# Pacing the second image's layer work by its matmuls in a selective-scan stack

## The chip, the core and the metric

The kernel runs on one core of one Trainium2 chip, in float32. The metric is the device time of one execution, in microseconds (us). A core has engines that run side by side and meet through semaphores: PE (TensorE, matmuls; its weight loads are the row PEld), DVE (VectorE), ACT (ScalarE), POOL (GpSimd) and SP (SyncE), which here only issues DMAs. Each engine works through its own list of instructions in the order in which the program wrote them.

## What is computed

Four layers run on an input of 4 images of 64 x 64 pixels and 128 channels. Layers 0, 1 and 3 are selective-scan blocks; layer 2 is a gated block without a scan. Cut to what matters, a scan layer is:

```python
xz = layer_norm(x) @ in_proj                      # 128 -> 2 x 256 channels: x_, z
xs = silu(conv3x3_depthwise(x_) + conv_b)         # read in 4 directions k: rows, columns, and both backwards
dts, B, C = split(x_proj[k] @ xs[k])              # 8 + 16 + 16 rows for each of the 4096 positions
delta = softplus(dt_w[k] @ dts + dt_b)
h[t] = exp(delta[t] * A) * h[t-1] + delta[t] * xs[t] * B[t]   # 256 channels x 16 states
y[t] = sum over the 16 states of h[t] * C[t]
x = x + out_proj @ (layer_norm(sum over k of y) * silu(z))
x = x + fc2 @ gelu(fc1 @ layer_norm(x))
```

The rest of this text calls the recurrence for h "the scan", delta * xs * B "the B product", and h * C "the C product".

## The kernel before, in words

**Turns.** Images are taken in pairs. Each image passes the three scan layers, which makes 12 turns (`turns`): images 0 and 1 through layer 0, then both through layer 1, then layer 3, then the same for images 2 and 3. A turn scans one image in one layer. It has 4 directions x 8 chunks of 512 positions = 32 chunks, and a chunk has 8 periods, each for 4 of the 16 states of one half of the channels. There are 12 x 32 x 8 = 3072 periods.

**A period.** In each period DVE runs 4 scans (L870), two of them fed by a B product that PE makes in PSUM (`pair_db`, L845, tile `dbp`) and two by products that DVE makes itself (L983, L984) from a copy `dv` that ACT lifts into PSUM (L862). ACT computes the decays `da` (L854) and the diagonal matrices `diag` (L837) that PE uses for the next B product. POOL multiplies by C (L882) and in every second period adds two results (L884). PE sums over the states into `yp` (L895). The rows of B and C come by DMA, broadcast to all partitions (`bb`, `cb`, L821), two buffers each. The B product of the next period stands in PE's list between the two halves of a period.

**The other image's work.** Everything else of a layer (the norms, the projections, the convolution by 9 matmuls for each half of the channels, the gated block) is done for the other image while this one is scanned, in PE, ACT, DVE and POOL slots between the scan's instructions. The function `between` writes it as a list S of small steps: one step is a matmul, or an activation, or a DMA, and empty steps (`rest`) stand where a result needs time to arrive. The list from layer 1 to layer 3 holds layer 2 too; it is called gated, it is the longest, it takes 3 taps of the convolution in one step where the other lists take 1, and it has fewer empty steps (`breath` is 0 in it, so that no empty step stands between `root`, `scale` and `affine` of a norm).

**The places.** A period has four places at which `other(number)` may run steps: after the first scan, after the second scan with PE's B product and sums, after the third scan, and at the end. A turn has 32 x 32 = 1024 places. A list is spread evenly: at each place `other` runs as many steps as the share of the list's length that the share of places gone by asks for. An empty step counts as one step, as does a step with three matmuls. Lists of the first chunks of the program and of the last 7 chunks and the tail are given one chunk each.

**Queues and buffers around it.** All matmul results of the other image go through one PSUM buffer (`gap`), so that a matmul waits until the result before it has been read. A norm is the chain `mean` (PE L226), `centre` (DVE L230), `square` (ACT L234), `variance` (PE L238), `root` (ACT L241, L242), `scale` (DVE L245), `affine` (ACT L252); the norm of y (L338 to L361) is like it. A convolution ends with ACT's `take` (L413), then comes `silu` (L421), which changes ACT's function table twice. Column stores (L430) and row stores (L435) stand in SP's list with the `bb` and `cb` loads.

Of the kernel before, what the change touches and what calls it, by code (L numbers as in the profile page):

```python
# [59 lines left out]
VSS_AT, VSS_N = _columns(_VSS)  # L60
GATE_AT, GATE_N = _columns(_GATE)


@with_exitstack
def vss_stack_kernel(ctx: ExitStack, tc: tile.TileContext, x: bass.AP, weights, out: bass.AP, n_batch=B, layers=(0, 1, 2, 3)):
# [90 lines left out]
    def combine(i, psums):  # L156
# [33 lines left out]
        for m in range(2):  # L190
            S.extend((partial(turn, m), take))
            for t in range(0, 9, 4):
                count = min(4, 9 - t)
                S.extend((partial(taps, m, t, count), partial(project, count), partial(leave, m, t, count)))
        return S

    def between(e, frm, to, psums):
# [10 lines left out]
        def rest(n=pause):  # L208

            S.extend([lambda: None] * n)  # L210

# [10 lines left out]
        def norm(src, dst, wgt, bias, eps):  # L222

            def mean():
                z.ps = bank()
                nc.tensor.matmul(z.ps, mean128, src(), start=True, stop=True)  # L226
# [5 lines left out]
            def square():  # L232
                z.sq = gap1.tile([P, CH], F32, tag="sq", name="sq")
                nc.scalar.activation(z.sq, z.cen, AF.Square)  # L234

            def variance():
                z.ps = bank()
                nc.tensor.matmul(z.ps, mean128, z.sq, start=True, stop=True)  # L238
# [70 lines left out]
        def begin(c):  # L309


            def turn():
                z.ps = bank()
                for j in range(4):
                    nc.tensor.transpose(z.ps[:, j * P : (j + 1) * P], z.xt[:, j, :], ident)

            def take():
                z.res = gap2.tile([P, CH], F32, tag="res", name="res")
                nc.scalar.copy(z.res, z.ps)

            S.append(turn)
            if c + 1 < NCH:
                S.append(lambda: fetch_x(c + 1))
            S.append(take)
            later(lambda: nc.sync.dma_start(out=lane.res[:, cols(c)], in_=z.res))

        def output_norm(c):
            if to is None:
                S.append(lambda: fetch(c))
                rest(2)  # L330

            def mean():
                z.y, z.res = z.next_y, z.next_res
# [9 lines left out]
            def square():  # L343
                z.wide = gap1.tile([P, 4, CH], F32, tag="wide", name="wide")
                nc.scalar.activation(z.wide[:, 0:2], z.y, AF.Square)

            def variance():
                z.ps = bank()
# [25 lines left out]

        def project_z():
            def first():
                z.ps = bank()
                nc.tensor.matmul(z.ps, z.in_z[:, :P], z.xn, start=True, stop=True)

            def second():  # L380
                z.ps = bank()
# [7 lines left out]
        def convolve(c):  # L389

            stride = 3 if gated else 1
            for m in range(2):
                for first in range(0, 9, stride):

                    def taps(m=m, first=first):
                        if m == 0 and first == 0 and (frm is None or gated):
# [46 lines left out]
        def mixer_out(c):  # L443
            def gate():
                nc.gpsimd.tensor_mul(z.y, z.y, z.wide[:, 0:2])

            def project():
                z.ps = bank()
# [16 lines left out]
        def mlp(c, store):  # L465
# [5 lines left out]
            for j in range(4):  # L471

                def up(j=j):
                    if j == 0:
# [15 lines left out]
            for j in range(4):  # L490

                def down(j=j):
                    if j == 0:
# [50 lines left out]

        def finish(c):
            def turn():
                z.ps = bank()
# [14 lines left out]
        def gate_sums(c):  # L562
# [7 lines left out]
            norm(lambda: z.res, fresh, g["n1w"], g["n1b"], eps6)  # L570

            def first():
                z.ps = bank()
                nc.tensor.matmul(z.ps, g["w1"][:, :P], z.t, start=True, stop=True)

            def take():
                z.g1 = gap1.tile([P, CH], F32, tag="cen", name="g1")
                nc.scalar.activation(z.g1, z.ps, AF.Identity, scale=g["wdw"][:, 0:1], bias=g["cb"][:, 0:1])

            def second():  # L580
                z.ps = bank()
# [17 lines left out]
        def attention():  # L599
            g = wt[2]  # L600

            def mean():
                z.mean = gap1.tile([P, 1], F32, tag="mean", name="mean")
                nc.vector.tensor_reduce(z.mean, z.sums, AX.X, ALU.add)
                nc.vector.tensor_scalar_mul(z.mean, z.mean, 1.0 / L)

            def se():
                z.ps = bank()
# [11 lines left out]
        def gate_rest(c):  # L620
            g = wt[2]

            def project():
                z.s, z.res = z.next_s, z.next_res
# [16 lines left out]
            norm(lambda: z.res, fresh, g["n2w"], g["n2b"], eps6)  # L641

            def first():
                z.ps = bank()
                nc.tensor.matmul(z.ps, g["wf1"][:, :P], z.t, start=True, stop=True)

            def take():
                z.c1 = gap1.tile([P, CH], F32, tag="cen", name="c1")
                nc.scalar.activation(z.c1, z.ps, AF.Identity, bias=g["bf1"][:, 0:1])

            def second():
                z.ps = bank()
                nc.tensor.matmul(z.ps, g["wf1"][:, P:], z.t, start=True, stop=True)

            def both():
                z.c2 = gap1.tile([P, CH], F32, tag="sq", name="c2")
                nc.vector.scalar_tensor_tensor(z.c2, z.ps, g["bf1"][:, 1:2], z.c1, ALU.add, ALU.mult)

            def down():
                z.ps = bank()  # L660
# [95 lines left out]
    def scans(pool, ring, deep, psum):  # L756
# [178 lines left out]
        for at, (s, i) in enumerate(periods):  # L935
            then = periods[at + 1] if at + 1 < len(periods) else None
            if i == 0:
# [4 lines left out]
                if at % (8 * per_turn) == 0:  # L942
                    segments = [(steps, len(steps), frm, to) for steps, frm, to in meanwhile(s.turn)]

# [5 lines left out]
            def other(number):  # L950

                gone = at % (8 * per_turn) * 4 + number
                for todo, count, frm, to in segments:
                    while todo and count - len(todo) < count * (gone - frm) / (to - frm):
                        todo.pop(0)()

# [48 lines left out]
            if then and then[0].turn != s.turn:  # L1005
                assert not any(todo for todo, *_ in segments)
        save(*before, 1)
        add_up(*before, 0)
        add_up(*before, 1)
        while full:  # L1010
            leave(*full.pop(0))
        for todo, *_ in segments:
            for step in todo:
                step()
# [93 lines left out]
```

## Time and profile before

| what | value |
|---|---|
| median of 3 runs | 22745.52 us (22731.7 to 22749.28) |
| the profiled execution | 22741.48 us |
| its span, first to last instruction | 22739.6 us |
| busy: PE, DVE, POOL, ACT | 19888.1, 19492.9, 19252.4, 18595.2 us (87, 86, 85, 82%) |
| before the first scan; after the last period's first scan, to the end | 164.9 us; 87.1 us |
| a chunk without work of the other image | 50.7 us |
| mean granted TensorE clock | 0.959 of full speed |

The page's rows give, for a group of instructions, its line, engine, operation and tiles (out<-in), the busy time and the mean ns of one, and then the idle time of the engine just before them with what ended it. A float32 matmul shows as two PE records. Because all four engines are busy for more than four fifths of the span, no single row names the limit; the waits between the engines do.

### The profile page before, as it was taken

To read this page: it belongs to the slowest core of one execution; us is meant where nothing else is said; L and a number is where in the kernel's file an instruction comes from. 1 tells how busy PE (TensorE), PEld (TensorE's weight loads), DVE (VectorE), ACT (ScalarE), POOL (GpSimd) and SP (SyncE) were. 2 spreads that over 40 slices of the span, in tenths; PEclk is the share of its full clock that TensorE was granted. 3 is DMA by queue.
4 is the path that set the end of the run, shared out by engine and by line. 5 is a ranking of instruction groups with operands and counts; after the bars stand their busy time and mean duration, and the time that the engine had idled before them with its cause. 6 is when DMAs were issued, how large, how long until landed. Compare 5 with 4: busy or idle time off the path is not lost. (4 is left out here: it accounts for less than half of the span.)

```text
span 22739.6 us, 217018 instructions
## 1 busy us (share of the span) xinstructions
PE 19888.1 (87%) x58234; PEld 10543.0 (46%) x58234; DVE 19492.9 (86%) x20186; ACT 18595.2 (82%) x40022; POOL 19252.4 (85%) x8862
## 2 busy tenths in 40 slices
PE   7898898898888888888888888888988888888887
PEld 3444444444444444444444444444444444444443
DVE  5999888888887887888899898898888878878996
ACT  5888888888887887788788788888888878878887
POOL 5999888888887887888889888898888878878996
PEclk8999999999999999999999999999999999999999
DMA  4444444444334434434533544444443443344333
GB/s 106 151 146 149 133 135 146 134 135 144 128 130 129 133 128 124 141 132 139 139 139 138 137 142 138 133 148 133 135 143 126 128 131 134 126 129 143 137 136 106
DMA packets 2437559, 3060.10 MB, mean 135 GB/s; under 512 B 1753840, under 2 KB 1790064, under 8 KB 2238192
## 3 DMA queue, kind: packets, MB, share of 16 engines
q1 hardware_dynamic: 2436336, 3046.22, 42.5%
q8 instruction: 472, 7.73, 0.1%
q14 instruction: 751, 6.15, 0.1%
HBM read 2784.41 MB, written 261.49 MB: 134 GB/s over the span
## 5 line engine op out<-in xcount | busy, mean ns | idle before, releaser
L882 POOL TENSOR_TENSOR hc<-h,cb 128x1024 f32<-128x1024 f32 x6144 | 14411.8, 2361 | 3101.8 <-DVE h L870 1904.4
L895 PE MATMUL yp<-hc,ident 128*128 128x512 f32 x18432 | 9102.8, 621 | 661.2 <-POOL hc L884 447.5
L854 ACT ACTIVATE da<-delta,w 128x512 f32<-128x512 f32 x12288 | 8149.0, 713 | 684.1 <-DVE h L870 671.8
L870 DVE TENSOR_TENSOR_SCAN h<-da,state,dbp 128x512 f32<-128x512 f32 x5376 | 6574.0, 1261 | 1384.8 <-PE dbp L845 1100.3
L845 PE MATMUL dbp<-diag,duT 128*128 128x256 f32 x24576 | 6143.1, 394 | 1314.4 <-DVE h L870 1178.4
L870 DVE TENSOR_TENSOR_SCAN h<-da,state,dv 128x512 f32<-128x512 f32 x5376 | 6585.5, 1263 | 0.0
L845 PEld LDWEIGHTS dbp<-diag,duT 128*128 128x128 f32 x24576 | 4686.5, 195 | 3725.0 <-issue 2165.5
L895 PEld LDWEIGHTS yp<-hc,ident 128*128 128x128 f32 x18432 | 3488.9, 197 | 5003.4 <-issue 3651.1
L837 ACT ACTIVATE diag<-ident,bt 128x128 f32<-128x128 f32 x12288 | 3952.1, 401 | 0.0
L884 POOL TENSOR_TENSOR hc<-hc 128x1024 f32<-128x1024 f32 x1536 | 3621.9, 2358 | 120.4
L983 DVE TENSOR_TENSOR dv<-dv,bb 128x512 f32<-128x512 f32 x3072 | 2087.0, 679 | 837.9 <-ACT dv L862 704.4
L862 ACT COPY dv<-du 128x512 f32<-128x512 f32 x3072 | 1799.9, 586 | 1137.5 <-DVE h L870 1129.4
L984 DVE TENSOR_TENSOR dv<-dv,bb 128x512 f32<-128x512 f32 x3072 | 2116.5, 689 | 0.0
L402 PE MATMUL gap<-halo,cw 128*128 128x512 f32 x3456 | 1657.1, 604 | 17.3 <-ACT wide L385 6.8
L870 DVE TENSOR_TENSOR_SCAN h<-da,dbp 128x512 f32<-128x512 f32 x768 | 893.5, 1201 | 203.1 <-PE dbp L845 166.5
L788 PE MATMUL ps_dt<-xd,dt_w 8*128 8x512 f32 x1536 | 888.7, 659 | 147.6 <-ACT delta L791 78.5
L805 POOL TENSOR_TENSOR du<-delta,xs 128x512 f32<-128x512 f32 x768 | 978.5, 1274 | 32.7 <-ACT delta L793 32.7
L402 PEld LDWEIGHTS gap<-halo,cw 128*128 128x128 f32 x3456 | 641.1, 192 | 743.9 <-issue 697.3
L878 ACT COPY state<-h 128x2 f32<-128x2 f32 x5376 | 964.6, 179 | 0.0
L870 DVE TENSOR_TENSOR_SCAN h<-da,dv 128x512 f32<-128x512 f32 x768 | 894.7, 1203 | 0.0
L413 ACT ACTIVATE wide<-gap,w 128x512 f32<-128x512 f32 x192 | 131.9, 687 | 826.1 <-PE gap L402 826.1
L813 ACT COPY duT<-ps_duT 128x512 f32<-128x512 f32 x768 | 440.9, 574 | 182.6 <-PE ps_duT L811 181.2
(122 smaller groups left out, 11955.2 us busy)
## 6 DMA issues: line engine op xcount, KB each, us to landing
cb<-xd_d SPq DMA_DIRECT2D x1536, 1024.0 KB
bb<-xd_d SPq DMA_DIRECT2D x1536, 512.0 KB
xs<-x_row_d SPq DMA_DIRECT2D x192, 512.0 KB
xs<-x_col_d SPq DMA_DIRECT2D x192, 512.0 KB
x_col_d<-down SPq DMA_DIRECT2D x192, 256.0 KB
x_row_d<-wide SPq DMA_DIRECT2D x96, 512.0 KB
y_d<-y_sb SPq DMA_DIRECT2D x96, 512.0 KB
y<-y_d SPq DMA_DIRECT2D x96, 512.0 KB
```

The lines of the kernel that those rows point to most:

```text
L402: nc.tensor.matmul(z.ps, z.cw[:, m, t, :], z.halo[c][:, dy : dy + RPC, dx : dx + W], start=(t == 0), stop=(t == 8),)
L805: nc.gpsimd.tensor_mul(s.du[:, m], s.delta[:, m], s.xs[:, m])
L837: nc.scalar.activation(s.diag[q][:, t, :, j], ident, AF.Copy, scale=s.bt[:, t, CQ * q + j : CQ * q + j + 1])
L845: nc.tensor.matmul(s.db[:, t * P : (t + 1) * P, :], s.duT[:, t, m, :], s.diag[q][:, t], start=True, stop=True)
L854: nc.scalar.activation(da[:, j], s.delta[:, m], AF.Exp, scale=s.v["a"][:, s.k, m, n : n + 1])
L862: nc.scalar.copy(dv[i % 2], s.du[:, place(s, i)[1]])
L870: nc.vector.tensor_tensor_scan(s.h[i, side][:, j, s.step], da[:, j, s.step], db[:, s.step], init, ALU.mult, ALU.add)
L882: nc.gpsimd.tensor_mul(hc, s.h[i, side], s.cb[i // 2][:, 2 * side : 2 * side + 2, :])
L884: nc.gpsimd.tensor_add(hc, hc, s.hc[i, 0])
L895: nc.tensor.matmul(getattr(s, f"yp{m}"), ident, s.hc[i, side][:, j], start=opens and j == 0, stop=i == end and side == 1 and j == 1,)
L983: nc.vector.tensor_mul(db, du, s.bb[i // 2][:, 0])
L984: nc.vector.tensor_mul(du, du, s.bb[i // 2][:, 1])
```

## The change

The steps are spread by cost and not by count. A decorator marks a step with the number of its matmuls; an unmarked step costs 0.25, an empty one 0.05. The share of places gone by is replaced by `when(place)`, in which the 8 periods of a chunk have the weights ROOM. After an empty step, or where the next step is of the other sort (with matmuls, without matmuls), a place ends even if the list is behind its share. Lists that are given a single chunk keep the old rule. The convolution of the gated list takes one tap in a step. No instruction is added or removed; only their order within each engine's list changes.

```diff
+ROOM = (3.2, 0.8, 2.5, 0.6, 1.6, 0.6, 2.2, 1.2)
+def tensor(matmuls):
+    def mark(fn):
+        fn.matmuls = matmuls
+        return fn
+    return mark
+def cost(step):
+    return getattr(step, "matmuls", 0) or (0.05 if step is empty else 0.25)
+def empty():
+    pass
+def alike(a, b):
+    return empty in (a, b) or hasattr(a, "matmuls") == hasattr(b, "matmuls")
+def when(place):
+    chunk, place = divmod(place - 1, 4 * len(ROOM))
+    i, number = divmod(place, 4)
+    return chunk + (sum(ROOM[:i]) + ROOM[i] * number / 4) / sum(ROOM)
...
-            S.extend([lambda: None] * n)
+            S.extend([empty] * n)
...
+            @tensor(1)
             def mean():
...
-            stride = 3 if gated else 1
+            stride = 1
...
+                    @tensor(stride)
                     def taps(m=m, first=first):
...
-                    segments = [(steps, len(steps), frm, to) for steps, frm, to in meanwhile(s.turn)]
+                    segments = [
+                        SimpleNamespace(todo=steps, done=0, dense=True, total=len(steps), frm=frm, to=to)
+                        if to - frm <= 4 * 8
+                        else SimpleNamespace(
+                            todo=steps, done=0, dense=False, total=sum(map(cost, steps)), frm=when(frm), to=when(to)
+                        )
+                        for steps, frm, to in meanwhile(s.turn)
+                    ]
...
-                gone = at % (8 * per_turn) * 4 + number
-                for todo, count, frm, to in segments:
-                    while todo and count - len(todo) < count * (gone - frm) / (to - frm):
-                        todo.pop(0)()
+                place = at % (8 * per_turn) * 4 + number
+                for g in segments:
+                    gone = place if g.dense else when(place)
+                    while g.todo and g.done < g.total * (gone - g.frm) / (g.to - g.frm):
+                        step = g.todo.pop(0)
+                        g.done += 1 if g.dense else cost(step)
+                        step()
+                        if gone < g.to and not g.dense and (step is empty or g.todo and not alike(step, g.todo[0])):
+                            break
```

The other steps with matmuls get marks in the same way: 2 for the two matmuls over y and for the output projection, 1 for each projection, 0.6 for four 128-column transposes, 0.1 for the one-column matmul of layer 2.

More of the change, by code (lines that the diff above doesn't have):

```diff
@@ L190, in combine @@
         for m in range(2):
-            S.extend((partial(turn, m), take))
+            S.extend((tensor(0.3)(partial(turn, m)), take))
             for t in range(0, 9, 4):
                 count = min(4, 9 - t)
-                S.extend((partial(taps, m, t, count), partial(project, count), partial(leave, m, t, count)))
+                S.extend((partial(taps, m, t, count), tensor(0.3 * count)(partial(project, count)), partial(leave, m, t, count)))
         return S
@@ L234, in square @@
                 nc.scalar.activation(z.sq, z.cen, AF.Square)
+            @tensor(1)
             def variance():
@@ L309, in begin @@
         def begin(c):
+            @tensor(0.6)
             def turn():
@@ L330, in output_norm @@
                 rest(2)
+            @tensor(2)
             def mean():
@@ L345, in square @@
                 nc.scalar.activation(z.wide[:, 0:2], z.y, AF.Square)
+            @tensor(2)
             def variance():
@@ L375, in project_z @@
         def project_z():
+            @tensor(1)
             def first():
@@ L378, in first @@
                 nc.tensor.matmul(z.ps, z.in_z[:, :P], z.xn, start=True, stop=True)
+            @tensor(1)
             def second():
@@ L445, in gate @@
                 nc.gpsimd.tensor_mul(z.y, z.y, z.wide[:, 0:2])
+            @tensor(2)
             def project():
@@ L471, in mlp @@
             for j in range(4):
+                @tensor(1)
                 def up(j=j):
@@ L490, in mlp @@
             for j in range(4):
+                @tensor(1)
                 def down(j=j):
@@ L545, in finish @@
         def finish(c):
+            @tensor(0.6)
             def turn():
@@ L570, in gate_sums @@
             norm(lambda: z.res, fresh, g["n1w"], g["n1b"], eps6)
+            @tensor(1)
             def first():
@@ L578, in take @@
                 nc.scalar.activation(z.g1, z.ps, AF.Identity, scale=g["wdw"][:, 0:1], bias=g["cb"][:, 0:1])
+            @tensor(1)
             def second():
@@ L605, in mean @@
                 nc.vector.tensor_scalar_mul(z.mean, z.mean, 1.0 / L)
+            @tensor(0.1)
             def se():
@@ L621, in gate_rest @@
             g = wt[2]
+            @tensor(1)
             def project():
@@ L641, in gate_rest @@
             norm(lambda: z.res, fresh, g["n2w"], g["n2b"], eps6)
+            @tensor(1)
             def first():
@@ L649, in take @@
                 nc.scalar.activation(z.c1, z.ps, AF.Identity, bias=g["bf1"][:, 0:1])
+            @tensor(1)
             def second():
@@ L657, in both @@
                 nc.vector.scalar_tensor_tensor(z.c2, z.ps, g["bf1"][:, 1:2], z.c1, ALU.add, ALU.mult)
+            @tensor(1)
             def down():
@@ L1005, in scans @@
             if then and then[0].turn != s.turn:
-                assert not any(todo for todo, *_ in segments)
+                assert not any(g.todo for g in segments)
         save(*before, 1)
@@ L1011, in scans @@
             leave(*full.pop(0))
-        for todo, *_ in segments:
-            for step in todo:
+        for g in segments:
+            for step in g.todo:
                 step()
```

## The prediction

> **What bounds the kernel now.** I first read the busy times by stage: a chunk with no work of the other image, then one turn of each sort (ordinary, gated, and the one that ends a pair of images).
>
> ```profile
> core 0: us, PE busy (x) PEld busy (x) DVE busy (x) ACT busy (x) POOL busy (x), PEclk, DMA share, GB/s
> 1902.80:1953.50 50.70, 43.85 (x132) 23.23 (x132) 48.46 (x51) 40.58 (x83) 49.17 (x23) 0.97 0.43 148
> 1953.50:3769.80 1816.30, 1611.19 (x4768) 857.67 (x4768) 1612.53 (x1665) 1511.87 (x3277) 1594.22 (x731) 0.97 0.44 138
> 5580.40:7559.00 1978.60, 1710.98 (x4930) 901.52 (x4930) 1645.82 (x1716) 1593.43 (x3400) 1624.35 (x755) 0.96 0.41 131
> 9545.50:11391.70 1846.20, 1638.29 (x4832) 872.21 (x4832) 1614.14 (x1665) 1535.09 (x3311) 1594.71 (x731) 0.96 0.44 138
> ```
>
> An empty chunk is bound by DVE and POOL together (48.5 and 49.2 of 50.7 us). DVE's work hardly differs between turns; its idle time does: 204 us in an ordinary turn, 333 in a gated one, 232 in the third. Over the span DVE idles 22739.6 - 19492.9 = 3247 us. As no instruction comes or goes, the change is worth what it does to this number. Next, the list of waits says what DVE, and the engines it waits for, wait on:
>
> ```profile
> DVE h L870 <- PE dbp L845: 1266.8, 658, 9.6
> ...
> ACT wide L413 <- PE gap L402: 826.1, 180, 10.2
> ...
> DVE dv L983 <- ACT dv L862: 704.4, 346, 6.4
> ...
> POOL hc L882 <- DMA cb<-xd_d: 368.1, 78, 10.9
> ...
> DVE cen L245 <- ACT gap L242: 290.2, 139, 10.7
> ```
>
> (us in all, times, longest.) Six tenths of DVE's idle time (1971 of 3247 us) are late B products and late copies `dv`. A timeline of a gated turn shows one late B product, first PE and then DVE:
>
> ```profile
> 7419.01 5.31 PE L402 MATMUL gap<-halo,cw 128*128 128x512 f32 x12
> 7424.16 1.88 PE L895 MATMUL yp<-hc,ident 128*128 128x512 f32 x4
> 7425.88 1.89 PE L845 MATMUL dbp<-diag,duT 128*128 128x256 f32 x8
> ```
>
> ```profile
> 7427.90 2.45 DVE L870 TENSOR_TENSOR_SCAN h<-da,state,dbp 128x512 f32<-128x512 f32 x2 [8.88 <-POOL hc L882]
> ```
>
> Six taps (12 records) hold PE for 5.31 us, 0.88 us each; the B product behind them ends at 7427.77, and the scan starts 0.13 us later after 8.88 us of idling (the row names POOL, but PE came last). The last wait of the list is of another sort, and in the same turn one case of it shows what the change will make common:
>
> ```profile
> 7328.53 1.02 PE L238 MATMUL gap<-sq,mean 128*128 128x512 f32 x2
> ...
> 7330.28 0.58 ACT L242 ACTIVATE gap<-gap 128x512 f32<-128x512 f32 x1
> ...
> 7330.90 0.69 DVE L245 TENSOR_TENSOR cen<-cen,gap 128x512 f32<-128x512 f32 x1 [3.56 <-ACT gap L242]
> 7331.50 1.27 DVE L870 TENSOR_TENSOR_SCAN h<-da,state,dv 128x512 f32<-128x512 f32 x1
> ```
>
> Here `root` (ACT) and `scale` (DVE) stand in the same place; ACT and PE run behind DVE, so DVE idles 3.56 us with a scan queued behind it.
>
> **Part 1, matmuls spread: a gain.** Stepping the two pacing formulas through all 12,288 places gives the matmuls that each period gets. From the trace I take DVE's idle time per period, without the waits of the other image's own DVE instructions, by the number of those matmuls in that period and the one before (2984 periods; the first chunk of the program and the last 7 chunks left out):
>
> 0 matmuls: 0.85 us (395 periods before, 265 after); 1 or 2: 0.37 (1593, 1256); 3 or 4: 0.72 (597, 1265); 5 to 8: 1.58 (323, 198); 9 or more: 5.11 (76, none).
>
> The sums are 2249 us before and 1912 after: a gain of 337. By the means of each sort of turn it is 292. The classes are coarse: a class of 3 or 4 before is often one clump, after it is spread. If instead each period of the new order takes the mean of the 12 old periods with the same number in the chunk and the most similar work in the two periods, the sum is 1328; the same method gives 1853 for the old order when each sort of turn is predicted from the others, so the gain by it is 525. I take 470, nearer the second, which sees clumps; the ends are 292 and 525.
>
> The size rests on 0.88 us for a float32 matmul of 512 columns. The Trainium skill ("TensorE: Matmul & The Clock Gate", "Back-to-back issue gap") speaks against it: warm matmuls of 512 columns follow each other every 216 ns. Even with two records to a product that is 0.43 us, six taps would hold PE for 2.6 us and not 5.31, and the gain would be half (235 us). The row decides. The same page ("HAM oscillation") lets the clock fall by half after pauses of some 3.4 us, which would make even spreading worth more; but the granted clock is 0.96 in the gated turn and 0.97 in the ordinary one, and 1% of 1711 us of PE in four turns is 68 us on an engine that seldom ends last. I count nothing for it.
>
> **Part 2, the last tap and `take` apart: a gain.** ACT idled 826 us for the last tap, in 180 waits: 6.9 us where `take` stood in the same place, 4.7 one place on, 1.3 two places on. The old order has 11, 141 and 36 of these, the new one 1, 73 and 55, and 59 still farther off. That leaves 7 + 343 + 72 = 422 us, so ACT gets about 370 us back, just before `silu`. Part of it sits in the 704 us in which DVE waits for `dv`. Between nothing and 250 us I take 120, a third.
>
> **Part 3, steps without matmuls packed: a cost.** Since an unmarked step costs only 0.25 and the place does not end between two of them, `root` and `scale` fall together wherever no empty step parts them, and elsewhere come one place closer. Mean wait of DVE by distance in places, with the counts before and after:
>
> `scale` L245: 3.53 us at 0 (4, 128), 1.59 at 1 (135, 98), 0.42 at 2 (65, 22), nothing beyond: 256 us become 617, +361. The 128 are all norms of the four gated turns.
> `scale` of y, L357: 3.61 at 0 (4, 24), 1.98 at 1 (35, 51), 0.48 at 2 (45, 16), 0.42 at 3 (11, 4): 110 become 197, +87.
> `centre` L230 behind `mean`: 0.44 at 2 (19, 115), 0.43 at 3 (88, 104), then nothing: +49.
> The sum over a chunk of layer 2, L592 behind POOL: 2.48 at 2 (32, 4); now 28 at 1, which the trace doesn't have. It costs at least 2.48, at most about a place more (7.4 us per period / 4 = 1.9): I take 4.4, +54.
> L341, L453 and L500 gain some 10.
>
> Together +541. The 3.5 us rest on 8 cases, but they fit: over all places ACT runs 0.7 to 2.4 us behind DVE and PE 0.5 to 4, and `root` itself takes 1.24. Not all is lost: while DVE stands, PE and ACT catch up. In the old trace a microsecond of such waits goes with 0.2 us less of the other waits in the same and the next two periods. So +430; the ends are +300 (if a PE with fewer clumps shortens the 3.5 to 2.4) and +541.
>
> Behind a waiting `scale` stand the scans; for these wait POOL's C products, then PE's sums.
>
> **Part 4, other queues.** SP: stores come one or two places closer to their producers (column store L430 behind ACT's `down`: mostly 2 places before, 1 after; row store L435: 4, now 2). SP waits in order, and the `bb` and `cb` loads stand behind. `cb` is issued 14.5 us ahead of its use when nothing stands between, but 9.1 us when a column store does, and those 138 cases hold 355 of POOL's 368 us of waiting. Losing one place of lead costs at most 138 x 1.5 = 200 us, at least nothing (POOL runs 2 to 5 us behind DVE): +40, since SP's lead is governed by the time of ACT's `down`, which the change also brings forward. PE: `down` of the MLP comes one place closer to `gelu`, the output projection closer to POOL's gate; PE waits up to 190 us more, of which a B product feels a part: +40, between 0 and 190. ACT waits more for DVE's `centre` (now in the same place, 237 of 251); ACT has 18% idle and mostly waits for DVE anyway: nothing, but up to 50 us if `dv` is late behind it. The weights ROOM move matmuls from periods 4 to 6 to periods 0 to 3, less than they say, since the empty steps hold the list back: nothing. Opening, last 7 chunks and tail keep their order.
>
> **Sum.** -470 - 120 + 430 + 40 + 40 = -80 us. Against the profiled 22741.5 (span 22739.6 and 1.9 around it) that is 22661; the median of the runs lies 4 us higher: 22665.
>
> **Rivals.** (A) The short distances win: `scale` waits its full 3.5 us in each gated norm. With +541, queues +100, the low gain of 292 and nothing from part 2: +349, 23095. It decides from the point where DVE's waits at L245 and L357 (404 us before) pass about 950. For it: eight measured cases and a count that is certain. Against: PE's clumps were part of why ACT was late. Chance 0.28. (B) Even spreading is worth all that the similar periods say, and shortens the `scale` waits as well: -525 - 250 + 300 + 20 = -455, 22290. For it: periods with 1 or 2 matmuls idle only 0.37 us. Against: each `silu` blocks ACT for some 3.7 us wherever it stands. Chance 0.27. (C) PE's lateness is set by POOL and DVE, on which its sums wait, and neither spreading nor packing is felt: 22745, chance 0.03. The forecast has 0.42.
>
> A measurement of this kernel can tell about 0.2% (45 us) from no change. The forecast's own uncertainty is about 150 us, so it splits 0.25, 0.09, 0.08 into faster, same, slower; A gives 0.27 slower and 0.01 same; B is faster; C the same. In all 0.52, 0.13, 0.35. The range 22350 to 22960 leaves out the outer part of A and of B.
>
> **What would show it.** Right if in the new profile DVE's wait for `dbp` falls from 1267 to some 800 to 900 us and ACT's for L402 from 826 to about 420, while L245 rises from 290 to about 600 and L357 from 114 to about 200; gated turns should stay near 1980 us and ordinary ones lose 10 to 20. Wrong if PE's clumps were not what made B products late (the `dbp` wait stays above 1100), or if `scale` in the same place costs DVE under 2 us, or if POOL's wait for `cb` passes 600 us.

## The result and the profile after

| | before | after |
|---|---|---|
| median of 8 runs | 22741.55 us (22729.28 to 22749.34) | 22681.33 us (22676.98 to 22686.12) |
| profiled span | 22739.6 us | 22682.3 us |
| busy: PE, DVE, POOL, ACT | 19888.1, 19492.9, 19252.4, 18595.2 us | 19815.6, 19497.9, 19246.5, 18647.2 us |
| mean granted TensorE clock | 0.959 | 0.956 |

The ratio is 0.9974 (95% interval 0.9963 to 0.9985): the changed kernel is 60 us faster, and the forecast was 80 us. The busy times moved by at most 73 us on any engine, so what changed is the waiting. In what follows every ratio is against the kernel before, run on the same chip, and a hundredth of it is 227 us. "Before" and "after" are the two given kernels, and an experiment is named by its label. Line numbers from L265 up to L1051 in rows of "after" are those of the changed kernel: its L923 is L870 of before, L281 is L245, L265 is L230, L396 is L357, L455 is L413, L444 is L402, L898 is L845, L915 is L862, L278 is L242, L472 is L430, L477 is L435, L496 is L453, L874 is L821, L935 is L882 and L1050 is L983.

The busy times by stage, of after, for the same four stages as before (an empty chunk, an ordinary, a gated and a third turn):

```profile
core 0: us, PE busy (x) PEld busy (x) DVE busy (x) ACT busy (x) POOL busy (x), PEclk, DMA share, GB/s
1931.60:1982.30 50.70, 43.87 (x132) 23.29 (x132) 48.44 (x52) 40.57 (x83) 49.17 (x23) 0.97 0.45 148
1982.30:3791.10 1808.80, 1606.91 (x4768) 863.29 (x4768) 1612.18 (x1665) 1513.45 (x3277) 1593.27 (x731) 0.96 0.44 138
5600.40:7587.30 1986.90, 1713.57 (x4930) 907.14 (x4930) 1647.93 (x1717) 1601.73 (x3400) 1624.63 (x755) 0.95 0.42 130
9570.60:11378.90 1808.30, 1615.89 (x4832) 868.47 (x4832) 1612.32 (x1665) 1539.51 (x3311) 1593.46 (x731) 0.97 0.45 141
```

The empty chunk is as long as before. The ordinary turn became 7 us shorter, the third 38 shorter, and the gated one 8 longer. The means over all turns of a sort, from the starts of the first scan of each turn (turn 11 runs to the end of the span), will carry the experiments:

| us per turn | before | after | breath1 | all0 | late_store | breath1_late | noend |
|---|---|---|---|---|---|---|---|
| ordinary (4 turns) | 1812.8 | 1809.1 | 1808.7 | 1842.2 | 1768.8 | 1767.9 | 1862.9 |
| gated (4) | 1983.1 | 1985.2 | 1929.7 | 1981.7 | 1967.8 | 1945.6 | 2049.5 |
| third (2) | 1839.6 | 1808.6 | 1809.0 | 1853.5 | 1800.7 | 1800.7 | 1850.1 |
| turn 0 | 1789 | 1819 | 1817 | 1829 | 1774 | 1773 | 1833 |
| turn 11 | 1923 | 1905 | 1903 | 1936 | 1906 | 1898 | 1933 |

The list of waits of after (us in all, times, longest):

```profile
DVE h L923 <- PE dbp L898: 1083.4, 715, 14.5
...
DVE dv L1050 <- ACT dv L915: 553.3, 276, 6.4
POOL hc L935 <- DMA cb<-xd_d: 550.4, 80, 14.3
DVE cen L281 <- ACT gap L278: 531.9, 206, 10.7
...
ACT wide L455 <- PE gap L444: 249.6, 97, 10.2
...
DVE res L496 <- PE gap L493: 126.2, 25, 13.5
```

The reader is to hold these against the rows of before. Late B products fell from 1267 to 1083 us, late copies `dv` from 704 to 553, and ACT's wait for the last tap from 826 to 250. In their place stand three rows that grew: POOL's wait for the C rows (368 to 550), DVE's wait for `root` at `scale` (290 to 532), and the residual's addition at L496 (34 to 126). The last of these is not among the rows of before shown so far:

```profile
DVE res L453 <- PE gap L450: 33.8, 11, 13.5
```

In a gated turn every single `scale` now waits. This is what the trace answers for the norm's tile in the gated turn that starts at 5600 us, the instruction's own row and the idle time ahead of the group:

```profile
L281 DVE TENSOR_TENSOR cen<-cen,gap x32: 686/686/689, 5685.6 to 7344.7; 128x512 f32<-128x512 f32 x32
...
its engine sat idle before it (us, times) until:
  ACT gap L278: 92.3, 32
```

32 norms, 32 waits, 92.3 / 32 = 2.88 us each. A timeline of DVE shows the first one, with a scan of the recurrence behind it that has all its inputs:

```profile
5682.40 1.27 DVE L923 TENSOR_TENSOR_SCAN h<-da,state,dv 128x512 f32<-128x512 f32 x1
5685.62 0.69 DVE L281 TENSOR_TENSOR cen<-cen,gap 128x512 f32<-128x512 f32 x1 [1.95 <-ACT gap L278]
5686.22 1.27 DVE L923 TENSOR_TENSOR_SCAN h<-da,state,dv 128x512 f32<-128x512 f32 x1
```

The product for that scan was ready at 5682.49 and its decays at about 5682.67, so by these rows DVE could have run it at 5683.67; it ran it at 5686.22. ACT had waited 1.56 us for PE's `variance` (ACT's row at 5684.31) before it spent 1.24 us on `root`: three engines pass one small result on, and DVE, which is ahead of both, pays for the whole path.

To set this against the prediction's sum I split DVE's idle time over the same 2984 periods in two. (They are the 3072 without the first four chunks and the last seven; the prediction says the first chunk.) Waits of the other image's own DVE instructions, from here on "own waits", went from 542 to 887 us (+345). All other waits went from 2249 to 1838 us (-411). The net is -66 us, beside -60 in the medians.

### The profile page after: what moved, and what is told of

It reads as the page before. It is cut to its first block, busy times and chain, and to the rows that moved or that the text cites. A ratio compares the mean times of both kernels' runs of the same rounds, so it can differ in the third digit from the quotient of the medians.

```text
span 22682.3 us, 216904 instructions
## 1 busy us (share of the span) xinstructions
PE 19815.6 (87%) x58234; PEld 10564.4 (47%) x58234; DVE 19497.9 (86%) x20186; ACT 18647.2 (82%) x40022; POOL 19246.5 (85%) x8862
## 5 line engine op out<-in xcount | busy, mean ns | idle before, releaser
L935 POOL TENSOR_TENSOR hc<-h,cb 128x1024 f32<-128x1024 f32 x6144 | 14406.9, 2362 | 2937.3 <-DVE h L923 1825.8
L923 DVE TENSOR_TENSOR_SCAN h<-da,state,dbp 128x512 f32<-128x512 f32 x5376 | 6569.2, 1261 | 1123.5 <-PE dbp L898 893.0
L898 PE MATMUL dbp<-diag,duT 128*128 128x256 f32 x24576 | 6105.1, 392 | 1014.8 <-DVE h L923 965.7
L923 DVE TENSOR_TENSOR_SCAN h<-da,state,dv 128x512 f32<-128x512 f32 x5376 | 6583.5, 1263 | 0.0
L898 PEld LDWEIGHTS dbp<-diag,duT 128*128 128x128 f32 x24576 | 4720.4, 195 | 3320.5 <-issue 2038.1
L915 ACT COPY dv<-du 128x512 f32<-128x512 f32 x3072 | 1800.2, 586 | 1208.3 <-DVE h L923 1202.0
L1050 DVE TENSOR_TENSOR dv<-dv,bb 128x512 f32<-128x512 f32 x3072 | 2083.0, 678 | 665.3 <-ACT dv L915 553.3
L1051 DVE TENSOR_TENSOR dv<-dv,bb 128x512 f32<-128x512 f32 x3072 | 2113.8, 688 | 0.0
L444 PE MATMUL gap<-halo,cw 128*128 128x512 f32 x3456 | 1757.2, 607 | 14.2 <-DVE cen L281 7.6
L923 DVE TENSOR_TENSOR_SCAN h<-da,dbp 128x512 f32<-128x512 f32 x768 | 893.4, 1201 | 236.8 <-PE dbp L898 190.4
L858 POOL TENSOR_TENSOR du<-delta,xs 128x512 f32<-128x512 f32 x768 | 979.0, 1275 | 32.8 <-ACT delta L846 32.8
L444 PEld LDWEIGHTS gap<-halo,cw 128*128 128x128 f32 x3456 | 631.4, 192 | 661.9 <-issue 605.6
L923 DVE TENSOR_TENSOR_SCAN h<-da,dv 128x512 f32<-128x512 f32 x768 | 892.6, 1201 | 0.0
L844 ACT ACTIVATE delta<-ps_dt,w 128x512 f32<-128x512 f32 x768 | 524.5, 683 | 215.9 <-PE ps_dt L841 211.0
L281 DVE TENSOR_TENSOR cen<-cen,gap 128x512 f32<-128x512 f32 x256 | 175.0, 684 | 533.0 <-ACT gap L278 531.9
```

Source lines behind the costliest of these rows:

```text
L444: nc.tensor.matmul(z.ps, z.cw[:, m, t, :], z.halo[c][:, dy : dy + RPC, dx : dx + W], start=(t == 0), stop=(t == 8),)
L858: nc.gpsimd.tensor_mul(s.du[:, m], s.delta[:, m], s.xs[:, m])
L898: nc.tensor.matmul(s.db[:, t * P : (t + 1) * P, :], s.duT[:, t, m, :], s.diag[q][:, t], start=True, stop=True)
L915: nc.scalar.copy(dv[i % 2], s.du[:, place(s, i)[1]])
L923: nc.vector.tensor_tensor_scan(s.h[i, side][:, j, s.step], da[:, j, s.step], db[:, s.step], init, ALU.mult, ALU.add)
L935: nc.gpsimd.tensor_mul(hc, s.h[i, side], s.cb[i // 2][:, 2 * side : 2 * side + 2, :])
```

## The experiments

The theory on trial: the change trades the lateness of PE and ACT, which spreading cures, for waits of consumers packed too close behind their producers; undo the packing and keep the spreading, and the gain that the packing hides comes out. The rival: the packing is harmless, because an engine that stands at a short distance would stand anyway.

**breath1** gives the gated list, in the changed kernel, the one empty step that the other lists have: ahead of `scale` and `affine` of both norms, and one step more between POOL's gate and PE's output projection and in one place of the MLP.

```diff
-        pause, breath, delayed = (2 if gated else 3), (0 if gated else 1), []
+        pause, breath, delayed = (2 if gated else 3), 1, []
```

> The changed kernel with one empty step put back between root, scale and affine of every norm of the gated list, nothing else. By the pacing formula scale (L281) then never stands in root's place: 128, 98, 22, 3 cases at distance 0, 1, 2, 3 become 0, 218, 30, 3; for y's norm 24, 51, 16, 4 become 0, 59, 32, 4. Theory (packed steps are a cost of their own): at the changed kernel's prices (2.88, 1.18, 0.47 us; 2.13, 0.71, 0.10) DVE's waits fall by 224 + 44 = 268 us, of which four fifths reach the end: about 22465 us, all of it in the four gated turns (1985 to some 1930 us each). Rival (a stalled DVE only lets PE and ACT catch up, so the waits move to the B product): L281 falls just the same, the wait for dbp rises by as much, 22650 to 22700 us.

Measured: 22476.25 us, ratio 0.9880 (0.9866 to 0.9893), so 214 us better than after, all of it in the gated turns (4 x 55.5 us). Its waits:

```profile
DVE h L923 <- PE dbp L898: 1041.6, 691, 14.6
...
DVE cen L281 <- ACT gap L278: 369.3, 179, 10.7
```

No `scale` stands in the place of its `root` any longer, and its wait falls by 163 us; ACT's wait at `affine` falls from 97 to 6 us, PE's behind POOL's gate from 103 to 65, and B products are 42 us less late. Split as above, own waits fall by 188 us and all others by 36: the waits did not move elsewhere, as the rival had it. Which of these distances carries how much of the 214 us is not separated. The packing is not harmless.

**all0** goes the other way: no empty step there in any list (`breath` is 0 throughout, the same line).

> The changed kernel with the empty steps between root, scale and affine taken out of all lists, as they are in the gated one: the suspected cost is made larger. Scale in root's place: 128 become 214. Theory: 86 more cases at 2.88 us in place of 1.18 or less, +156 us at L281 and +28 at y's norm, four fifths of it at the end: about 22830 us; the ordinary turns, 1809 us, become some 1825 to 1830 us, the gated ones stay. Rival (waits only move): 22680 us, with the wait for dbp lower by what L281 gains.

Measured: 22933.37 us, ratio 1.0082 (1.0068 to 1.0096), 245 us worse than after; the effect has the expected direction and is some 100 us larger. The gated turns, whose list is unchanged, take 1982 us; an ordinary one takes 33 more and a third 45 more. `scale` waits 754 us (+222, with 86 more norms in the same place as their `root`), y's `scale` 33 more, and the `dbp` row rises by 120 to 1204. Own waits rise by 202 us and all others by 31: nothing was given back by a catching up of the other engines.

**b_stride1** takes only the single taps of the gated list into the kernel before, with its pacing by count (`stride = 1`); **taps3** takes them out of the changed kernel (`stride = 3 if gated else 1`).

> The kernel before with one change, single taps in the gated list, still spread by count. Theory: single taps alone do little, since the list is then longer (more steps at each place): periods with 9 or more matmuls in two periods go from 76 only to 48, those with 5 to 8 rise from 327 to 399; by the means of before -22 us. The longer list packs root and scale (4 cases in the same place become 40): +70 us. About 22780 us. Rival (three taps in one step are themselves what hurts, not their density): 28 clump periods fewer at some 4.7 us and every remaining one shorter, 22600 us or less.

> The changed kernel with the three taps of the gated list in one step again (cost 3), paced by cost as before. Density is the same: classes of 0, 1-2, 3-4, 5-8, 9+ matmuls in two periods 281, 1215, 1272, 212, 4 against 265, 1235, 1280, 204, 0. Theory (density makes the gain, not the size of a step): at the changed kernel's means +15 us, scale's distances are unchanged, 22690 us. Rival (three taps together, 2.6 us of PE ahead of a B product, are what hurts): 96 triples in each of 4 turns, some half of them ahead of a B product at 1 us or more, +150 to +200 us, 22850 us, with the wait for dbp above 1200 us.

Measured: 22742.4 us, ratio 1.0001 (0.9993 to 1.001), and 22667.26 us, ratio 0.9974 (0.9965 to 0.9983). Neither can be told from its parent; the 40 us that b_stride1 was expected to lose are not there either (its `scale` row rose by 22 us, not by 70). Whether a clump of three taps is cut into single steps does not matter here, under either pacing.

**noend** removes the rule that an empty step or a change of sort ends a place:

```diff
-                        if gone < g.to and not g.dense and (step is empty or g.todo and not alike(step, g.todo[0])):
-                            break
```

> The changed kernel without the rule that an empty step or a change of engine ends a place: pacing by cost and ROOM alone. The matmuls are spread as in the changed kernel (classes of 0, 1-2, 3-4, 5-8 matmuls: 249, 1217, 1330, 188 periods). Theory: the ends only guard the distances between steps that wait for each other; without them centre stands one place behind mean in 52 norms, y's scale in root's place in 46 cases for 24, the channel sums in POOL's place 24 times, column stores in their producer's place 107 times for 10: +150 us, about 22830 us. Rival (the ends only hold the list back and cost spread): 22680 us or less.

Measured: 23284.47 us, ratio 1.0237 (1.0223 to 1.0251), 450 us beyond what I expected. Its waits:

```profile
DVE h L923 <- PE dbp L898: 1263.2, 783, 13.3
...
POOL hc L935 <- DMA cb<-xd_d: 684.4, 80, 17.3
...
DVE cen L281 <- ACT gap L278: 428.4, 206, 10.7
...
DVE cen L265 <- PE gap L261: 413.5, 105, 31.9
```

Without the ends an empty step, which costs only 0.05, parts next to nothing: `centre` comes one place behind its `mean` in 52 cases, at 4.5 us each, and its row goes from 132 to 413 us; B products are as late as in the kernel before, and C rows are later than ever. Yet the matmuls are spread as in after, with no two neighbouring periods that hold nine or more: even spreading does not by itself make B products early. Pacing by cost alone would have been a loss of 2.4%; the rule that ends a place is worth some 600 us and is what makes the change a gain at all.

**flat** sets all weights of the eight periods to 1 (`ROOM = (1.0,) * 8`).

> The changed kernel with ROOM set to 1 for all 8 periods of a chunk. Classes 259, 1157, 1447, 121, 0: at the changed kernel's means the same sum (1836 us against 1838). Scale at 0, 1, 2 places: 128, 109, 14 (before 128, 98, 22), y's scale 4, 64, 27 (24, 51, 16), the channel sums two places off in all 32 cases (28 were at one), the last tap's take one place off only 27 times (73). Theory (ROOM is worth nothing, distances are): -20 to -70 us, about 22640 us. Rival (the weights put matmuls where PE has room between B products): dbp waits rise by 100 us or more, 22780 us.

Measured: 22722.75 us, ratio 0.9997 (0.9989 to 1.0005): 52 us worse than after, and I had expected a gain. B products are not the reason (1064 us of waiting, 1083 in after). One of its rows:

```profile
DVE dv L1050 <- DMA bb<-xd_d: 214.8, 64, 7.8
```

DVE waits 215 us for rows of B, where after has 105. Ordinary turns are 12 us shorter without the weights and gated ones 15 longer. What the weights do is thus not what their name in the change suggests; that they keep the other image's DMAs out of the way of the B rows is a reading of these rows, not shown.

The list of after has one more row that had grown, the C rows. It led to the second set. Ahead of each column store stands one empty step; **late_store** makes it three in the changed kernel, and nothing else:

```diff
-                rest(1)
+                rest(3)
                 S.extend((lambda: store(0), lambda: turn(1)))
-                rest(1)
+                rest(3)
                 S.append(lambda: store(1))
```

> The changed kernel with two more empty steps ahead of each column store: the store stands mostly 3 places behind its producer (before 1), the row store 2 or 3 (2). Theory (the closer stores hold SP and cost the C rows their lead): POOL's wait for cb falls from 550 us to 370 or less, where the kernel before had it, and half of that reaches the end; the longer list gives some back (5-8 matmuls: 245 periods for 204, +15 us; scale in root's place 116 for 128, -20 us): about 22590 us. Rival (POOL's wait for cb is covered by its own lag, or follows the transfer and not the place of its issue): cb wait or time unchanged, 22660 to 22700 us.

Measured: 22374.36 us, ratio 0.9846 (0.9833 to 0.986), 291 us better than after. I had expected a third of that. POOL's wait for C rows and two others, of late_store:

```profile
DVE h L923 <- PE dbp L898: 971.1, 682, 8.1
...
DVE cen L281 <- ACT gap L278: 454.9, 203, 9.1
POOL hc L935 <- DMA cb<-xd_d: 275.2, 81, 9.6
```

And SP's own waits at the column store, first of after, then of late_store, then of before:

```profile
SPq L472 <- ACT down L468: 1448.9, 106, 29.3
```

```profile
SPq L472 <- ACT down L468: 355.2, 135, 7.2
```

```profile
SPq L430 <- ACT down L426: 2017.0, 130, 30.2
```

SP spent 1449 us standing in front of a store whose data ACT had not yet copied. In the kernel before (the last row) it was more, 2017 us, with less waiting for C rows: the length of the standing is not what grew. SP usually runs a buffer ahead of the scan, so that it reaches the store long before its data exist, and the loads behind it lose their lead. A timeline of SP in after (start, duration, line) shows the worst form:

```profile
2347.02 0.32 SPq L874 DMA_DIRECT2D cb<-xd_d  x1
2367.46 0.37 SPq L472 DMA_DIRECT2D x_col_d<-down  x1
2367.88 4.51 SPq L477 DMA_DIRECT2D x_row_d<-wide  x1
2372.49 0.56 SPq L874 DMA_DIRECT2D bb<-xd_d  x1
2373.09 0.99 SPq L472 DMA_DIRECT2D x_col_d<-down  x1
2374.18 6.82 SPq L874 DMA_DIRECT2D cb<-xd_d  x1
```

For 20 us nothing is issued; then three stores (1 MB) go out with the next rows of B between them, and the C rows last. POOL gets them 10.00 us late:

```profile
2385.97 4.67 POOL L935 TENSOR_TENSOR hc<-h,cb 128x1024 f32<-128x1024 f32 x2 [10.00 <-DMA cb<-xd_d]
```

A count over the trace makes it general. C rows with all three stores of a chunk between them and the C rows before: 51 in before, with 189 us of POOL's waiting; 77 in after, with 433 of its 550 us; 52 in late_store, with 156 us. The likely reason is that steps without matmuls are now packed, and each such bunch also costs more (189 / 51 = 3.7 us, 433 / 77 = 5.6; 156 / 52 = 3.0 in late_store). The standing itself is not gone in late_store: the row store is now the first in SP's list, and SP stands 920 us before it (a row that after does not have), which makes 1275 us of both. What the later stores bring is, on this count, that loads of B and C rows come out between them more often. This is not all of the 291 us: of the fall in DVE's idle time 208 us are other waits, and 89 us are own waits, which may come from the longer list, as it moves other steps too.

**store_only** asks whether it is the store or ACT's copy `turn(1)`, which late_store moves too: the copy stays one place behind the first one, only the stores go back (each copy gets a name of its own for that).

```diff
                 rest(1)
-                S.extend((lambda: store(0), lambda: turn(1)))
-                rest(1)
+                S.append(lambda: turn(1))
+                rest(2)
+                S.append(lambda: store(0))
+                rest(3)
                 S.append(lambda: store(1))
```

> The stores of the run late_store, with ACT's two copies ahead of them left one place apart as in the changed kernel (there they moved apart by two places as well). The list has the same length. Theory (it is the store, waiting at the head of SP's list with the loads of B and C rows behind it, that costs): POOL's wait for cb 300 us or less, time as in late_store, 22340 to 22420 us. Rival (it was ACT that gained, by having its two 1.1 us copies farther behind the 3.7 us of silu): cb wait falls too, time 22550 us or more.

Measured: 22404.09 us, ratio 0.9852 (0.9836 to 0.9867), with 281 us of waiting for C rows. It is not ACT's copy. That it is the store and not the list, which is four empty steps a chunk longer in both runs, is likely, as POOL's wait for C rows falls by 269 us, but no run has the longer list with the stores in their old place.

**breath2** puts two empty steps before `scale` and `affine` in every list of the changed kernel (`breath` is 2).

> The changed kernel with two empty steps between root, scale and affine in every list (changed kernel: 1, and 0 in the gated one; the earlier run: 1 in all). Scale then stands two places behind root in 217 cases, one in 7; y's scale never nearer than two. Theory: L281 falls to 217 x 0.46 + 10 = 110 us and 30 at the start (369 in the earlier run), y's scale to 30 or less (77); the longer list packs matmuls denser (1422, 1011, 235, 32 periods with 1-2, 3-4, 5-8, 9+), about +60 us: -290 x 0.8 + 60 against 22476, about 22300 us. Rival (distance two has no more to give because ACT and PE are then late elsewhere, and the dense stretches cost what they did before the change): 22450 us or more.

Measured: 22521.53 us, ratio 0.9910 (0.9896 to 0.9923), 0.3% worse than breath1 and far from what I expected. Its waits:

```profile
DVE h L923 <- PE dbp L898: 1114.6, 666, 11.1
...
DVE dv L1050 <- ACT dv L915: 683.7, 305, 7.7
...
DVE cen L281 <- ACT gap L278: 95.5, 63, 10.7
```

The wait at `scale` is all but gone (369 to 96 us), and the time does not follow: the empty steps take places, 32 periods now see nine or more matmuls in themselves and the period before (none in after and in breath1), and B products and copies are late instead: against breath1 own waits fall by 147 us and all others rise by 207. By these rows distance is bought with density.

**breath1_late** joins the two mends in the changed kernel; **b_late** and **b_breath1_late** make the late store alone, and both, in the kernel before.

> The changed kernel with both mends, the empty step between root, scale and affine of the gated list and the later column stores. Theory (two separate costs): the gains add, 22680 - 205 - 305 = 22170 us, gated turns about 1912 us, L281 about 330 us, cb wait about 280 us. Rival (both free the same idle time of PE and ACT, or the longer list makes clumps again: 20 periods with 9 or more matmuls): 22300 us or more.

> The kernel before (spread by count) with the two more empty steps ahead of each column store: mostly 4 places behind its producer, 2 before. Theory (stores held SP in the kernel before as well, the change made it worse): SP's hold at L430, 2017 us, falls to some hundreds, POOL's wait for cb from 368 to 200 us or less, time 22740 - 150 to 250, about 22550 us. Rival (the cost came with the change alone): 22700 to 22760 us.

> The kernel before with both mends, still spread by count: the same two repairs without the change. Scale one place behind root in 63 cases and two in 157 (before 135 and 65). Theory (spreading matmuls by cost is worth the 411 us that the other waits of DVE lost, when nothing takes it back): it stays 250 us or more above breath1_late, about 22450 us, with the waits for dbp near 1250 and ACT's for the last tap near 800 us. Rival (the change's spreading is worth little once steps keep their distances): within 80 us of breath1_late.

Measured:

| | ratio to before | us |
|---|---|---|
| breath1_late | 0.9803 (0.9789 to 0.9816) | 22289.19 |
| b_late | 0.9950 (0.9937 to 0.9962) | 22632.55 |
| b_breath1_late | 0.9875 (0.9861 to 0.9888) | 22458.28 |

breath1_late is the fastest of all. Its rows beside those of after:

```profile
DVE h L923 <- PE dbp L898: 1000.9, 683, 7.3
...
DVE cen L281 <- ACT gap L278: 372.4, 169, 9.1
...
POOL hc L935 <- DMA cb<-xd_d: 273.0, 88, 12.3
```

Both waits have fallen as far as each mend brings them alone, yet the gains do not add: 0.0094 + 0.0128 = 0.0222 apart, 0.0171 together, a shortfall of 116 us, which is beyond the intervals of the ratios; the time is near what the rival expected (22300 us). The shortfall sits in the gated turns: 1945.6 us, where breath1 alone has 1929.7. That list is longer by both mends, and 20 periods see nine or more matmuls (none with either mend alone), so breath2's limit is the likely reason; no run separates it.

The three also give the worth of the pacing by itself. With both mends on either side, pacing by count takes 0.9875 and pacing by cost 0.9803: 0.0072, or 164 us, nearly three times what the change as made brought. The 250 us and more that were expected here did not come, because the mends do not stop the packing: between these two kernels the other waits fall by 457 us, and own waits still rise by 277. The late store is worth 114 us in the kernel before (150 to 250 were expected) and 291 in the changed one, though POOL's wait for C rows falls by about as much in both (368 to 111, 550 to 275): in the kernel before the gain is less than half of that fall, in the changed one it is all of it and a little more, of which the 89 us of own waits are a part. Why stays open; longer single waits (5.6 against 3.7 us) are one candidate, fewer other delays to hide behind another.

## Why the prediction was right, and what was off in it

The time was met to 16 us, but by two errors of one size. The sum said: own waits of the other image's DVE steps +541, everything else -618 (470 and 120 gained, 40 and 40 lost in queues, and a fifth of 541 given back). The trace says +345 and -411. Each side was half again too large, and they cancel. The mechanism, a gain from spreading and `take` that the packing nearly eats up, is what the runs show; that the difference came out so near is luck.

**Part 1, spreading (470).** The gain is there, and it was overrated: the other waits of the four ordinary turns together fell from 746 to 632 us, of the gated ones from 882 to 684, of the two third ones from 425 to 324. With part 2, the queues and what was to be given back it brought 411 where the sum had 618. How much of this is part 1 is not separated, because late C rows, which part 4 underrated, are also in the 411. The nearest measurement is the pair with both mends, where stores are late on both sides: other waits fall by 457 us there, and parts 1 and 2 had 590. `dbp` fell to 1083, not to 800 or 900. taps3 and b_stride1 agree that the size of a step does not count. What the prediction did not have is that the gain hangs on the ends of the places: it took them as given in the counting of places and never priced them, and noend, with the same spreading of matmuls, has `dbp` at 1263. So the number of matmuls near a period, on which the 470 rest, does not alone set how late its B product is.

With the 216 ns per matmul that the prediction quotes from the Trainium skill ("TensorE: Matmul & The Clock Gate", "Back-to-back issue gap"; the section means an isolated matmul and has 131 ns for a sustained stream), which would have halved this part, the everything-else side of the sum would have been -383 instead of -618, and the trace has -411. That is no vote for 216 ns: the rows hold 0.88 us for a float32 product, so the duration of a matmul is not why part 1 came out small. But it shows that a sum met by the wrong number is not evidence either way.

The clock was read too lightly. Its mean hardly moved (0.959 before, 0.956 after), but the records of the granted clock in the trace know only full and half: in after it stood at half for 2009 us in all, in before for 1856. The rule on pauses of some 3.4 us that the prediction quotes agrees with them. Of the 148 pauses of PE of 3.4 us or more that began at full clock in after, 146 ran into a stretch at half clock that began in them or within 3.4 us behind them; of 521 pauses of 1 to 2 us, 43 did. At half clock the records of a B product start 427 ns apart, at full clock 216. In noend the half clock takes 2694 us, so a part of that kernel's loss may be the clock; no run separates it.

**Part 2, last tap and `take` apart (120).** ACT's wait for L402 fell to 250 us and not to 422, and the wait for `dv` by 151. The counts of distances were right; the price per distance fell (2.5 us one place on, where before had 4.7; 0.34 two on, 1.3 before). In b_breath1_late, where nothing of the pacing is changed, it is still 837. What it is worth in time is not separated from part 1 by any run.

**Part 3, packing (+541, of which 430).** This is the mis-sized term. In parts, predicted and measured: `scale` +361, +242 (128 at 2.88 us instead of 3.53, and 98 at 1.18 instead of 1.59); y's `scale` +87, -21 (24 at 2.13 instead of 3.61, 51 at 0.71 instead of 1.98); `centre` +49, +48; the sum of layer 2 +54, +28; the residual's addition L496 counted as a small gain, +92; two others (L379 and L545) gained 46. The counts of distances were right. The prices came from the old order and fell in the new one. The effect that the prediction named for its low end, that a PE with fewer clumps passes `variance` on sooner, fits (ACT's wait for `variance` fell from 284 to 180 us) but was not tested by itself. The fifth that was to come back elsewhere is not seen: own and other waits rise together in all0 and fall together in breath1.

**Part 4, queues (+40 and +40).** The named cost was there, with the named mechanism, and the estimate for SP was too low. POOL's wait for C rows rose by 182 us, inside the bound of 200, while the sum took 40. The reason given for so little, that ACT's `down` comes forward too, holds for SP's standing, which fell from 2017 to 1449 us, but that did not decide: three stores now stand in one bunch more often, and the prediction moved each store by its own distance and did not ask which stores meet between two C loads. It also shows in the turns: turn 0, which the prediction did not look at by itself, got 30 us longer; with late stores it takes 1774 us, 15 less than before. For PE, the output projection came closer to POOL's gate as said: PE's wait there rose from 44 to 103 us, inside the bound of 190, and L496, which waits for that projection, is up by 92. The weights ROOM were put at nothing and are worth 52 us.

**The marks that were named.** `dbp` at 1083: short of the 800 to 900, and just under the 1100 that would have refuted part 1. The other two signs of being wrong did not come either: `scale` in the same place costs 2.88 us (under 2 was the mark), and the C rows cost 550 us (600). L281 at 532 of 600, L396 at 94 of 200, L455 at 250 of 420, gated turns 1985 of 1980; ordinary turns lost 4 and not 10 to 20, while the third lost 31. Rival A would have had all of the +541 and 292 of the gain; its cost was overrated like the forecast's. Rival B's sum, 455 us faster, is close to what breath1_late reaches (448), but that kernel has the late store and a longer gated list as well, and pacing by itself was worth 164 us there: the likeness is no proof of B.

## What to carry to other kernels

When steps are moved by a cost model, list for each producer and consumer on different engines how many slots lie between them before and after, and price each distance from the trace; here one empty step more between such steps of one list, most of them in its norms, gave 0.94%, more than three times what the new order gave as made. Look at the issue queue in the same way: ask which stores come to stand between two loads that something waits for, and set stores so that such loads can go out between them (1.28% here, for four empty steps a chunk). And test such mends together: here their gains did not add.

## What the runs showed of the hardware

An issuing engine that stands before one store holds everything behind it: in after SP stood 1449 us before column stores in 106 waits, up to 29.3 us at a time. And issues that follow a store are slow: the 107 loads of B and C rows that SP issued within 2 us behind a store took it 6.45 us each at the median, the other 2965 took 0.32. The row store took 4.53 us right behind a column store, and 0.56 in late_store, where it goes first.

An elementwise instruction of 0.69 us on DVE, set in the same slot as the ACT instruction that feeds it, cost 2.88 us of DVE's waiting on average (128 cases in after). Waits of this sort came back in full in the kernel's time (all0: 202 us more of own waits, 245 us of time), though every engine idles for over a tenth of the span.

A mean granted clock of 0.956 can hide 2009 us at half clock, in 367 stretches of 5.5 us on average; nearly every pause of PE of 3.4 us or more ran into one.
